# Expert loads, high-part casts, first sums and two split groups in a Macaron–Mamba–MoE kernel

## The chip, the cores and the metric

The kernel runs on one core of one Trainium2 chip. The metric is device microseconds (us) from the start to the end of the program on that core. Engines are named as in the profile: PE (matrix products), DVE (VectorE), ACT (ScalarE), POOL (GpSimd), SP (the queue that issues DMAs).

## The reference

The input x has 4 sequences of 1024 tokens with 128 features. Three residual steps follow each other, each on a layer norm of x: half a mixture of experts, a Mamba block, and the same mixture again.

```python
x = x + 0.5 * ffn(layernorm(x))
x = x + mamba(layernorm(x))
x = x + 0.5 * ffn(layernorm(x))

def ffn(x):                      # E = 8 experts, H = 128, F = 512, all of them run
    p = softmax(x @ w_router); q = softmax(x @ w_gating / 0.1)
    h = silu(x @ w_gate[e]) * (x @ w_up[e])          # for every e
    cw = p * q; cw = cw / (sum(cw) + 1e-9)
    return sum_e(cw[e] * (h @ w_down[e]))
```

The Mamba block projects to 256 channels, convolves over 4 tokens, makes step sizes and B and C from the result, runs a recurrence with 16 states per channel along the tokens, gates and projects back. All matrices are float32.

## The kernel before, in words

The 4096 tokens are cut into 8 blocks of 512. There are 16 mixture stages (8 blocks, twice) and 8 Mamba stages. `order` (L231) lists the mixture stages: the first mixture of block 0, of block 1, of block 2, and so on, mixed with second mixtures later. The Mamba work of a block runs beside the mixture of later blocks.

A mixture stage is 8 **groups**, one per expert; the groups are numbered through, so group 9 is expert 1 of the second stage. A group is two **halves** of 256 hidden features. This text names a half by the number in its tile names: half 0_8 is the one whose tiles are `pg`, `pu` and `h_0_8`, in block 0; expert 0 is halves 0_0 and 0_2, expert 2 is 0_8 and 0_10, expert 7 is 0_28 and 0_30; block 1 goes from 1_0 on. For each half:

- **gate** (`gate_part`, L595, and `half_products`, L628): 6 matmuls into the PSUM tile `pg`. Every float32 weight is kept as a high part `wh` and a low part `wl` in a faster format, as is the input (`xh`, `xl`). A product is `wh` by `xh`, `wh` by `xl`, `wl` by `xh` (L641 to L643). ACT then takes the silu of `pg` into `h` (L625).
- **up** (`up_part`, L646): 6 matmuls into `pu`, and DVE multiplies `h` by `pu` (L657). `pg` and `pu` have one buffer each: the next gate waits for the silu, the next up for the product.
- **down** (`down`, L676): in an ordinary group two plain float32 matmuls by `wd` (L722). A group listed in `SPL` (L41) is **split**: ACT casts `h` to a high part `hh` (L665), DVE subtracts to get `hl` (L667), the weight `wd` is parted in the same way into `wds` (L610 on ACT, L612 on DVE), and six fast matmuls (L697, L705) take the place of the two. `SPL` holds groups 1 to 10 and 113 to 126.

After a group's last down, ACT copies the PSUM tile `pd` to SBUF (`take`, L730, L735), and its result is multiplied by the routing weight `cwb` (L744) and added to `acc` (L747). The groups below `OWN` = 9 do that on DVE, later ones on POOL. `cwb` comes by DMA (`load_cw`, L584) from a DRAM tile `cd` that `cwt` (L553) writes after a transpose on PE (L556); it has 3 buffers, so the load of the fourth waits for the multiplication by the first.

**Weights.** `load_expert` (L276) issues three DMAs on SP for one expert, `w_gate` and `w_up` into `raw`, `w_down` into `wd`. `raw` has one buffer for experts 0, 3, 6 and two for the others, so expert 3 waits until `raw` of expert 0 has been read, expert 4 until that of expert 1 has. `split_expert` (L296) casts `raw` to `wh` (L298) and subtracts to get `wl` (L299), both on DVE.

**What sets the order.** The program has no loop at run time. While it is built, a class `Plan` (L54) keeps estimated clocks of the engines, and every instruction of the five queues is written out in the order that it decides. Time is counted in slots, 8 to a group. Lists of events have a slot each; line L1180 puts the load of expert e at `WL` = -5 slots and its parting at `WS` = +1 slot from slot 8(e-1). DVE work that may wait is handed to `plan.put` and taken when the planned DVE is free before the planned PE needs it; ACT work goes to `plan.act_put`. `plan.need` and `plan.act_need` force what has not yet been placed. Each queue runs in its order: an instruction that waits holds up all behind it on the same engine. A wait that the planner does not foresee is not avoided by it. `LOCK` (L47) and `on_pool` (L78) hold a model in which some DVE instructions and the POOL instructions exclude each other.

Around the change the layer norm of block 1 matters too (`mean_on_act`, L369): ACT sums (L379) and squares (L392), POOL makes `rs` and `nb` (L397 to L399), ACT writes `xn` (L414), PE transposes it (L438), ACT and DVE make `xh` and `xl` (L466, L471).

Of the kernel before, what the change touches and what calls it, by code (L numbers as in the profile page):

```python
# [8 lines left out]
F32 = mybir.dt.float32  # L9
F32R = mybir.dt.float32r  # L10
AF = mybir.ActivationFunctionType
ALU = mybir.AluOpType
# [25 lines left out]
POW = 4  # L38
WL = -5
WS = 1  # L40
SPL = (*range(1, 11), *range(113, 127))  # L41
OWN = 9
CWT0 = 11
FENDS = {0: 8, 1: 9, 9: 9, 15: 8}
# [128 lines left out]
def tile_macaron_mamba_moe(  # L173
# [20 lines left out]
    V, G, S, T = nc.vector, nc.gpsimd, nc.scalar, nc.tensor  # L194

    NB, L, H = x_in.shape
    E, _, F = w_gate.shape
# [20 lines left out]
    plan = Plan()  # L218
# [4 lines left out]
    def misc(name):  # L223
        if plan.reader in plan.spare:
            plan.act_need(plan.reader)
        plan.need(lambda: plan.reader is None or plan.reader[3])
        plan.wait_bank(name)
        return ps.tile([P, TB], F32, tag="misc", bufs=1, name=name)

    assert NBLK == 8  # L230
    order = [(1, 0), (1, 1), (1, 2), (1, 3), (2, 0), (1, 4), (2, 1), (1, 5), (2, 2), (1, 6), (1, 7)]  # L231
# [20 lines left out]
    def load_router():  # L252
        nc.sync.dma_start(out=wrg[:, 0:E], in_=w_router)
        nc.sync.dma_start(out=wrg[:, E:NE2], in_=w_gating)
# [16 lines left out]
        V.tensor_copy(wrg_h, wrg)  # L271
        V.tensor_tensor(wrg_l, wrg, wrg_h.bitcast(F32), ALU.subtract)

    wh, wl, wd, raws, cast = {}, {}, {}, {}, {}

    def load_expert(e):  # L276
        tag, bufs = (("xc", 1), ("y", 2))[e % 3 > 0]
        raw = sb.tile([P, 2, F], F32, tag=tag, bufs=bufs, name=f"wraw_{e}")
        nc.sync.dma_start(out=raw[:, 0, :], in_=w_gate[e])
        nc.sync.dma_start(out=raw[:, 1, :], in_=w_up[e])  # L280
        if e == 0:
            load_router()
        wd[e] = const.tile([P, FC * H], F32, name=f"wd_{e}")
        nc.sync.dma_start(
            out=wd[e].rearrange("p (c h) -> p c h", c=FC),
            in_=w_down[e].rearrange("(c p) h -> p c h", p=P),
        )
        wh[e] = const.tile([P, 2, F], F32R, name=f"wh_{e}")
        wl[e] = const.tile([P, 2, F], F32R, name=f"wl_{e}")
        raws[e] = raw  # L290
# [4 lines left out]

    def split_expert(e):  # L296
        raw = raws.pop(e)
        plan.put(lambda: V.tensor_copy(wh[e], raw), 0.69, plan.pe)  # L298
        cast[e] = plan.put(lambda: V.tensor_tensor(wl[e], raw, wh[e].bitcast(F32), ALU.subtract), 1.21, plan.pe)  # L299

    win_h = const.tile([P, 2 * DI], F32R, name="win_h")
    win_l = const.tile([P, 2 * DI], F32R, name="win_l")
# [289 lines left out]
    def split(s, e):  # L592
        return s * E + e in SPL

    def gate_part(s, c):  # L595
        d = ffn[s]
        kind, k = order[s]
        e, f = divmod(c, FC)
        assert e not in raws
        plan.need(lambda: "xl" in d)  # L600
        if e in cast:
            plan.need(lambda: cast[e][3])
        nm = f"{kind}_{k}_{c}"
        if f == 2 and s * E + e + 1 in SPL:
            x = (e + 1) % E
            ws = wds[s * E + e + 1] = {}
            ws["w"] = sb.tile([P, 2, FC * H], F32R, tag="big", bufs=BIG, name=f"wds_{s}_{e}")

            def high():
                S.copy(ws["w"][:, 0, :], wd[x])  # L610
                ws["wl"] = plan.put(
                    lambda: V.tensor_tensor(ws["w"][:, 1, :], wd[x], ws["w"][:, 0, :].bitcast(F32), ALU.subtract), 0.66, plan.act + 0.1  # L612
                )

            ws["wh"] = plan.act_put(high, 0.58, 0.0)
        g = s * GPS * FC + c
        pg = d["pg"] = half_products(s, c, 0, "pg", nm)
        t = plan.on_pe(1.38, silu_at.get(g - 2, 0.0))
        plan.act_fill(t + TOL - (1.29 if plan.table != "silu" else 0.0))
        if f == FC - 2:  # L620
            for w in list(ffn.values()):
                if "take" in w:
                    plan.act_need(w["take"])
        h = d["hp"] = sb.tile([P, 2, TB], F32, tag="h", bufs=HB, name=f"h_{nm}")
        S.activation(h, pg, AF.Silu)  # L625
        silu_at[g] = plan.on_act(1.06, t, "silu")
# [49 lines left out]
    def down(s, c):  # L676
        d = ffn[s]
        kind, k = order[s]
        e, f = divmod(c, FC)
        if f == 0:  # L680
            for o in list(ffn.values()):
                if "take" in o:
                    plan.act_need(o["take"])
            d["pd"] = ps.tile([P, TB], F32, tag="pd", bufs=1, name=f"pd_{kind}_{k}_{e}")
            if (s, e) == (len(order) - 1, E - 1):
                d["pds"] = d["pd"], misc("pd_end")
        h = d.pop(("h", c))
        cols = slice(f * H, (f + 1) * H)
        if len(h) == 2:
            ws = wds[s * E + e]  # L690
            w = ws["w"]
            if f % 2 == 0:
                plan.act_need(ws["wh"], d["hh", c])
                plan.need(lambda: ws["wl"][3])
                for q in range(2):
                    for i in range(2):
                        T.matmul(  # L697
                            d["pd"], w[:, i, (f + q) * H : (f + q + 1) * H], h[0][:, q, :],
                            start=(f + q + i == 0), stop=False,
                        )  # L700
                t = plan.on_pe(0.92, max(d["hh", c][4], ws["wl"][4]))
            else:
                plan.need(lambda: d["hl", c][3])
                for q in range(2):
                    T.matmul(  # L705
                        d["pd"], w[:, 0, (f + q - 1) * H : (f + q) * H], h[1][:, q, :],
                        start=False, stop=(f == FC - 1 and q == 1),
                    )
                t = plan.on_pe(0.46, d["hl", c][4])
        elif (s, e) == (len(order) - 1, E - 1):  # L710
            d["rest"] = d.get("rest", ()) + h
            if f % 2:
                for q in range(2):
                    part = slice(q * TB // 2, (q + 1) * TB // 2)
                    for g in (f - 1, f):
                        T.matmul(
                            d["pds"][q][:, 0 : TB // 2], wd[e][:, g * H : (g + 1) * H], d["rest"][g][:, part],
                            start=(g == 0), stop=(g == FC - 1),
                        )
            t = plan.on_pe(0.86, d["h_at", c])  # L720
        else:
            T.matmul(d["pd"], wd[e][:, cols], h[0], start=(f == 0), stop=(f == FC - 1))  # L722
            t = plan.on_pe(0.86, d["h_at", c])
        if f < FC - 1:
            return
        pd = d["pd"]
        edge = (s, e) == (len(order) - 1, E - 1)
        own = s * E + e < OWN or s == len(order) - 1

        def take():  # L730
            if e == 0:
                t = d["acc"] = sb.tile([P, TB], F32, tag="acc", bufs=2, name=f"acc_{kind}_{k}")
            else:
                t = sb.tile([P, TB], F32, tag="tmp", bufs=TMP, name=f"tmp_{kind}_{k}_{e}")
            S.copy(t, pd)  # L735

            def weight():
                cwb = d.pop(("cwb", e))
                at = max(plan.act, d["cwb_at", e])
                if e + 2 < E:  # L740
                    load_cw(s, e + 2)
                G_ = V if own else G
                put = (lambda f, cost, at: plan.put(f, 0.66, at)) if own else pool_put
                it = put(lambda: G_.tensor_tensor(t, t, cwb, ALU.mult), 1.25, at)  # L744
                if e > 0:
                    acc = d["acc"]
                    it = put(lambda: G_.tensor_tensor(acc, acc, t, ALU.add), 1.25, at)  # L747
                d["sum"] = it
                if e == E - 1:
                    d["tail"] = True  # L750
                    pool_run(None)

            if ("cwb", e) in d:
                weight()
            else:
                d.setdefault("late", []).append(weight)

        if edge:
            finish(d, d["pds"], k)
        else:  # L760
            d["take"] = plan.act_put(take, 0.58, t, True)
# [387 lines left out]
    def add(base, evs, wait=WAIT):  # L1149
        chains.append([(max(0, base + ev[0]), wait, *ev[1:]) for ev in evs])  # L1150
# [26 lines left out]
        add(START[k], mid, 99)  # L1177
        add(START[k], back, 40)
    for e in range(1, E):
        add(8 * (e - 1), [(WL, lambda e=e: load_expert(e)), (WS, lambda e=e: split_expert(e))])  # L1180
    add(8 * E, [(-24, load_mamba)])

    S.preload_act_table_set("silu_and_others")
# [3 lines left out]
    with tc.manual_schedule(engines={ET.PE, ET.Activation, ET.DVE, ET.Pool, ET.SP}):  # L1187
        half = 0
        while chains or done < nst:
            c = 2 * half  # L1190
            todo = []
            while done < min(nst, c - 2 * (done // FC in SPL)):
                todo.append(done)
# [47 lines left out]
```

## Time and profile before

| | us |
|---|---|
| three runs | 1262.1, 1262.14, 1264.05 |
| median | 1262.14 |
| the profiled execution | 1264.02 |
| its span, first to last instruction | 1262.2 |
| PE busy in the span | 1245.7 |
| DVE, ACT, POOL busy | 1141.8, 920.8, 705.8 |

The granted TensorE clock is full throughout. A matmul of 512 columns stands with 390 to 400 ns in the profile, but the next one starts 0.23 us later, because they overlap in the pipe. So the busy share of PE does not say how full it is: one looks at the starts. Twelve products and six split downs, one half of a split group, take 4.08 us from start to start where nothing waits; a half of an ordinary group takes 4.48 us. What a stretch takes beyond such steps is time that PE lost.

### The profile page before, as it was taken

The page shows a single profiled execution, that of the slowest core. Times are in us where ns is not written, and L with a number is a line of the kernel's source. Part 1 is how long each engine was busy: PE and PEld are TensorE (multiplying, and loading weights), DVE is VectorE, ACT ScalarE, POOL GpSimd, SP SyncE. Part 2 cuts the span into 40 slices and gives each one's busy share as a digit, 9 for nine tenths or more (in the row PEclk, how much of TensorE's full clock was granted, in tenths as well). Part 3 has the DMA queues.
Part 4 walks back from the last instruction along what each step waited for, and adds up shares of the span by engine and source line. Part 5 has one row for each costly group of instructions (what it writes and reads, how often), then busy time and mean ns, then how long its engine had stood idle before and what let it go on. Part 6 is the DMA issues. An engine that isn't in the chain of part 4 may idle for free. (4 is left out here: it accounts for less than half of the span.)

```text
span 1262.2 us, 14418 instructions
## 1 busy us (share of the span) xinstructions
PE 1245.7 (99%) x4800; PEld 861.0 (68%) x4800; DVE 1141.8 (90%) x1286; ACT 920.8 (73%) x1324; POOL 705.8 (56%) x557
## 2 busy tenths in 40 slices
PE   9999999999999999999999999999999999999998
PEld 6777666666666666666666666666666666667887
DVE  5986599999999999999999999999999999998676
ACT  6676887776778678877788787767876867656653
POOL 1012465767557656874576568656866575564400
PEclk9999999999999999999999999999999999999999
DMA  4501333243333433333433343433433433311110
GB/s 135 171 24 36 103 109 90 88 127 86 96 95 92 120 89 95 96 102 104 99 97 99 92 113 95 113 84 86 109 96 90 110 97 112 100 60 40 29 42 25
DMA packets 75387, 115.09 MB, mean 91 GB/s; under 512 B 7473, under 2 KB 23729, under 8 KB 75313
## 3 DMA queue, kind: packets, MB, share of 16 engines
q1 hardware_dynamic: 75312, 114.19, 33.4%
q8 instruction: 37, 0.61, 0.2%
q14 instruction: 38, 0.30, 0.1%
HBM read 109.71 MB, written 4.46 MB: 90 GB/s over the span
## 5 line engine op out<-in xcount | busy, mean ns | idle before, releaser
L722 PE MATMUL pd<-h,wd 128*128 128x512 f32 x824 | 391.5, 592 | 0.0
L657 DVE TENSOR_TENSOR h<-h,pu 128x1024 f32<-128x1024 f32 x256 | 310.9, 1214 | 69.8 <-PE pu L643 44.2
L1036 POOL TENSOR_TENSOR y_m<-y_m,da_m 128x1024 f32<-128x1024 f32 x128 | 309.7, 2420 | 107.6 <-DVE hb_m L1015 97.0
L625 ACT ACTIVATE h<-pg 128x1024 f32<-128x1024 f32 x256 | 262.9, 1027 | 139.4 <-PE pg L643 134.0
L641 PE MATMUL pg<-xh_f,wh 128*128 128x512 f32 x510 | 263.1, 516 | 1.5 <-DVE wh L298 0.7
L744 POOL TENSOR_TENSOR tmp<-tmp,cwb 128x512 f32<-128x512 f32 x98 | 132.1, 1348 | 206.2 <-issue 79.3
L722 PEld LDWEIGHTS pd<-h,wd 128*128 128x128 f32 x824 | 153.8, 188 | 107.0 <-issue 89.9
L641 PE MATMUL pu<-xh_f,wh 128*128 128x512 f32 x512 | 204.5, 399 | 2.5 <-DVE h L657 2.2
L643 PE MATMUL pg<-xh_f,wl 128*128 128x512 f32 x510 | 201.1, 394 | 0.5 <-DVE wl L299 0.5
L643 PE MATMUL pu<-xh_f,wl 128*128 128x512 f32 x512 | 200.4, 391 | 0.0
L642 PE MATMUL pu<-xl_f,wh 128*128 128x512 f32 x512 | 199.9, 390 | 0.0
L642 PE MATMUL pg<-xl_f,wh 128*128 128x512 f32 x510 | 199.4, 391 | 0.0
L1015 DVE TENSOR_TENSOR hb_m<-dx_m,bcb_m 128x1024 f32<-128x1024 f32 x128 | 173.2, 1353 | 2.2
L1021 DVE TENSOR_TENSOR_SCAN hb_m<-da_m,st_sb,hb_m 128x512 f32<-128x512 f32 x128 | 164.3, 1283 | 2.4
L1002 ACT ACTIVATE da_m<-dt_m,A_sb 128x512 f32<-128x512 f32 x256 | 164.0, 711 | 0.6
L1021 DVE TENSOR_TENSOR_SCAN hb_m<-da_m,hb_m 128x512 f32<-128x512 f32 x128 | 156.5, 1223 | 2.6
L1033 DVE TENSOR_TENSOR da_m<-hb_m,bcb_m 128x1024 f32<-128x1024 f32 x128 | 155.8, 1217 | 2.1
L641 PEld LDWEIGHTS pg<-xh_f,wh 128*128 128x128 f32 x510 | 96.0, 188 | 66.2 <-issue 26.8
L747 POOL TENSOR_TENSOR acc<-acc,tmp 128x512 f32<-128x512 f32 x98 | 130.2, 1329 | 7.7
L642 PEld LDWEIGHTS pg<-xl_f,wh 128*128 128x128 f32 x510 | 96.3, 189 | 46.8 <-issue 32.5
L641 PEld LDWEIGHTS pu<-xh_f,wh 128*128 128x128 f32 x512 | 96.1, 188 | 31.2 <-DVE h L657 11.5
L643 PEld LDWEIGHTS pg<-xh_f,wl 128*128 128x128 f32 x510 | 95.6, 188 | 23.0 <-DVE wl L299 0.9
(181 smaller groups left out, 1488.8 us busy)
## 6 DMA issues: line engine op xcount, KB each, us to landing
bcb_m<-bc_m SPq DMA_DIRECT2D x128, 512.0 KB
cwb<-cd_f SPq DMA_DIRECT2D x128, 256.0 KB
out_dram<-x SPq DMA_DIRECT2D x13, 256.0 KB
x<-in_L_attn_x_dram SPq DMA_DIRECT2D x8, 256.0 KB
wraw<-in_L_ffn_w_gate_dram SPq DMA_DIRECT2D x8, 256.0 KB
wraw<-in_L_ffn_w_up_dram SPq DMA_DIRECT2D x8, 256.0 KB
wd<-in_L_ffn_w_down_dram SPq DMA_DIRECT2D x8, 256.0 KB
cd_f<-ct_f SPq DMA_DIRECT2D x64, 4.0 KB
```

The costliest lines, as they stand in the source:

```text
L625: S.activation(h, pg, AF.Silu)
L641: T.matmul(o[:, q, :], wh[e][:, i, cols[q]], d["xh"], start=True, stop=False)
L642: T.matmul(o[:, q, :], wh[e][:, i, cols[q]], d["xl"], start=False, stop=False)
L643: T.matmul(o[:, q, :], wl[e][:, i, cols[q]], d["xh"], start=False, stop=True)
L657: V.tensor_tensor(h, h, pu, ALU.mult)
L722: T.matmul(d["pd"], wd[e][:, cols], h[0], start=(f == 0), stop=(f == FC - 1))
L744: it = put(lambda: G_.tensor_tensor(t, t, cwb, ALU.mult), 1.25, at)
L1002: S.activation(da[:, i, :], d["dt"][:, i, :], AF.Exp, scale=A_sb[:, i, n : n + 1])
L1015: mul = V.tensor_tensor(hb, d["dx"], bcb[:, 0:1, :].to_broadcast([P, ND, TB]), ALU.mult)
L1021: V.tensor_tensor_scan(hb[:, i, :], da[:, i, :], hb[:, i, :], 0.0 if first else st_sb[:, i, n : n + 1], ALU.mult, ALU.add,)
L1033: V.tensor_tensor(da, hb, bcb[:, 1:2, :].to_broadcast([P, ND, TB]), ALU.mult)
L1036: it = pool_put(lambda: G.tensor_tensor(d["y"], d["y"], da, ALU.add), 2.4, plan.dve)
```

## The change

Four things, in the code: expert 3 is loaded at -8 slots and expert 4 at -14 (both were at -5); a loaded expert's high part `wh` is cast by ACT and no longer by DVE, and only when that has been placed is the subtraction handed to DVE; of the groups below 9 only 7 and 8 keep their sums on DVE, so those of groups 0 to 6 go to POOL; groups 11 and 12 (experts 3 and 4 of block 1) are split as well. Two `need` lines keep the order right: a load of expert e above 3 is issued after the parting of expert e-3, and a gate forces the cast.

```diff
-SPL = (*range(1, 11), *range(113, 127))
+AHEAD = {3: -8, 4: -14, 5: -5, 6: -5}
+SPL = (*range(1, 13), *range(113, 127))
...
     def load_expert(e):
         tag, bufs = (("xc", 1), ("y", 2))[e % 3 > 0]
+        if e > 3:
+            plan.need(lambda: cast[e - 3] and cast[e - 3][3])
...
     def split_expert(e):
         raw = raws.pop(e)
-        plan.put(lambda: V.tensor_copy(wh[e], raw), 0.69, plan.pe)
-        cast[e] = plan.put(lambda: V.tensor_tensor(wl[e], raw, wh[e].bitcast(F32), ALU.subtract), 1.21, plan.pe)
+        def high():
+            S.copy(wh[e], raw)
+            cast[e] = plan.put(
+                lambda: V.tensor_tensor(wl[e], raw, wh[e].bitcast(F32), ALU.subtract), 1.21, plan.act + 0.1
+            )
+
+        cast[e] = None
+        high_at[e] = plan.act_put(high, 1.05, plan.pe)
...
         if e in cast:
+            plan.act_need(high_at[e])
             plan.need(lambda: cast[e][3])
...
-        own = s * E + e < OWN or s == len(order) - 1
+        own = (OWN - 3 < s * E + e < OWN) or s == len(order) - 1
...
-        add(8 * (e - 1), [(WL, lambda e=e: load_expert(e)), (WS, lambda e=e: split_expert(e))])
+        add(8 * (e - 1), [(AHEAD.get(e, WL), lambda e=e: load_expert(e)), (WS, lambda e=e: split_expert(e))])
```

Written out, the two programs have the same order on every engine from about the third stage on (some 230 us into the profile of before). Before that point it differs: 7 casts move from DVE to ACT, 13 instructions of the sums (7 multiplications, 6 additions) from DVE to POOL, and groups 11 and 12 add 6 casts on ACT, 6 subtractions on DVE, and 24 fast matmuls in place of 8 plain ones.

More of the change, by code (lines that the diff above doesn't have):

```diff
@@ L272, in split_router @@
         V.tensor_tensor(wrg_l, wrg, wrg_h.bitcast(F32), ALU.subtract)
-    wh, wl, wd, raws, cast = {}, {}, {}, {}, {}
+    wh, wl, wd, raws, cast, high_at = {}, {}, {}, {}, {}, {}
     def load_expert(e):
         tag, bufs = (("xc", 1), ("y", 2))[e % 3 > 0]
+        if e > 3:
+            plan.need(lambda: cast[e - 3] and cast[e - 3][3])
         raw = sb.tile([P, 2, F], F32, tag=tag, bufs=bufs, name=f"wraw_{e}")
```

## The prediction, made before the result was known

> **What bounds the kernel.** First the page's table of engines, then PE's waits in the first 230 us (below it the changed order is the old one), then windows.
>
> ```profile
> PE 1245.7 (99%) x4800; PEld 861.0 (68%) x4800; DVE 1141.8 (90%) x1286; ACT 920.8 (73%) x1324; POOL 705.8 (56%) x557
> ```
>
> PE is the bound from end to end: what PE loses, the program loses. The waits name where (us in total, times, longest):
>
> ```profile
> PE pd L705 <- DVE hl L667: 3.5, 2, 1.9
> ...
> PE pg L641 <- DVE wh L298: 0.7, 1, 0.7
> ...
> PE pg L643 <- DVE wl L299: 0.5, 1, 0.5
> ```
>
> All three name DVE, in stages 0 and 1. The windows (length, then busy us of each engine) show the stretches that I cut at gate starts:
>
> ```profile
> 24.36:40.34 15.98, 13.68 (x59) 10.32 (x59) 11.77 (x12) 9.09 (x14) 0.00 (x0) 1.00 0.66 214
> 40.34:66.15 25.81, 25.81 (x117) 21.08 (x115) 25.36 (x31) 17.58 (x24) 0.00 (x0) 1.00 0.48 128
> 66.15:82.00 15.85, 13.06 (x55) 9.90 (x54) 13.29 (x19) 12.70 (x23) 1.96 (x4) 1.00 0.05 17
> 82.00:113.79 31.79, 31.79 (x147) 25.86 (x145) 25.00 (x35) 23.59 (x41) 9.21 (x14) 1.00 0.16 50
> 113.79:148.76 34.97, 34.01 (x124) 22.10 (x123) 17.39 (x23) 22.92 (x31) 10.53 (x12) 1.00 0.28 79
> ```
>
> The reader sees DVE full in the second row (25.36 of 25.81) and POOL with nothing to do up to 66 us. Row one holds three halves, 12.69 us of work with a transposition of 0.45, so PE loses 3.3. Row three is three halves of 4.08: PE loses 3.6. The first loss starts with a late transfer (timelines of SP, DVE and PE; start, length):
>
> ```profile
> 26.31 0.37 SPq L279 DMA_DIRECT2D wraw<-in_L_ffn_w_gate_dram  x1
> ```
> ```profile
> 32.09 0.69 DVE L298 CAST wh<-wraw 128x1024 fp32r<-128x1024 f32 x1 [1.42 <-DMA wraw<-in_L_ffn_w_up_dram]
> ```
> ```profile
> 35.23 0.73 PE L705 MATMUL pd<-hl,wds 128*128 128x512 f32 x2 [1.91 <-DVE hl L667]
> ```
>
> Expert 3's load stood behind the write of `cd`, issued at 21.23 after a wait for ACT; DVE waits for it, and `hl` behind it makes PE wait.
>
> **Part 1, the early loads and the casts: 24 to 50 us.** I followed the changed order by hand with the durations above and these: silu 1.03, cast on ACT 1.05 (the row of `hh`, same shape; next start 0.95 later), product 1.22 (next 1.13 later), subtraction 1.23. Expert 3 can now be issued when `wl` of expert 0 ends (10.2), expert 4 after `wl` of expert 1 (15.1), both before `cd` at 21.2, so the transfers cost PE nothing. Expert 4's wait holds SP to 15.1, and three issues of 0.45 later SP is free for `cd`, which starts when it did.
>
> But the casts come late, because a forced cast is written just before its gate. ACT's first cast (expert 1, 11.6 to 12.6) fits: the exponentials behind it wait for DVE until 13.9 anyway. For expert 2 ACT's order is silu of half 0_6, then `wh`. ACT is full from 15.6, so that silu runs at about 23.7 (it was 23.2), the cast ends at 25.7, DVE's product 0_6 comes first and `wl` ends at 27.2. PE wants it at 24.84: a loss of **2.5**, of which 0.35 was lost before. Gate 0_10 starts at 30.9 (it was 28.80).
>
> Next a queue: on POOL the norm of block 1 (L397 to L399) now stands behind the first multiplication by `cwb`, which lands at 28.8 (DVE waited for it till then). POOL: 28.8 + 1.3, then 0.3 + 1.1 + 0.3 gives `nb` at 31.8, up to 33.0 if DVE's `wds` and `hl` hold it up. On ACT two `xn` wait for `nb`, and behind them the silu of 0_10, ready at 32.5: it ends at 33.9 to 34.9, then `wh` of expert 3, DVE's product 0_10, and `wl` at 36.3 to 37.3. PE wants it at 35.5: **0.9 to 1.8** lost. Gate 0_14 starts at 40.5 to 41.4 (40.34 before). From expert 4 on, the cast stands half a group ahead of its gate and nothing waits; the second gate of expert 4 starts at 49.8 to 50.7 against 49.70. The sum of the part: the loss of 3.3 goes, 3.3 to 4.3 take its place. I take **+0.5**. Bounds: -3.3, if no cast makes PE wait, to +1.9.
>
> **Part 2, DVE relieved: 50 to 82 us.** In a group of 8.16 us DVE had two products and two `hl` (4 x 1.13), `wl` 1.13, `wds` 0.60, `wh` 0.61, sums 1.33: 8.2, full. It loses 1.94. PE's 3.6 came from the order this forced: `wh` of expert 7 at 70.28 straight before its gate at 70.2, and `hl` of 0_26 after product 0_30 (80.16). Now `wh` of expert 7 stands two halves ahead, and `hl` of 0_26 before product 0_30: by hand at 76.5 for a need at 78.4. Gain 3.6, less 0.2 for product 0_30, which ends as up 1_0 wants it: **-3.4**; bounds -3.6 and 0.
>
> [...]
>
> ```profile
> 118.77 1.28 POOL L747 TENSOR_TENSOR acc<-acc,tmp 128x512 f32<-128x512 f32 x1
> ```
> ```profile
> 119.30 1.30 DVE L931 SCALAR_TENSOR_TENSOR cv_m<-xs_m,cw_sb,cv_m 128x512 f32<-128x512 f32 x1
> ```
>
> The DVE instruction takes 0.75 elsewhere and here 0.55 more: POOL ended at 120.05. At 109.63 it is POOL (1.84 for 1.30, against `hl`); the products of that time keep 1.22. POOL's two instructions a group, 2.6, meet `hl`, `wl`, `wds` (4.0 a group). DVE has 6.3 + waits of 0 to 2.6 in 8.16. In both rows a meeting costs about 0.55; I take two a group, 1.1: 7.4 of 8.16 fits.
>
> [...]
>
> POOL's new work stands ahead of the routing weights of block 1 (L547), and PE's transposition L556 is now written ahead of gate 1_2. By hand L547 ends at 82.6, PE comes at 83.0: **0**, bounds 0 and +1.3 (one sum held up).
>
> **Part 3, two split groups.** A half's down takes 1.36 for 1.72 (4.08 against 4.48 from start to start, the plain halves' pipe apart): four halves, **-1.44**. ACT gets 4 x 0.95 + 2 x 0.5, DVE 4 x 1.13 + 2 x 0.6 more; DVE is busy 17.39 of 34.97 there, ACT 22.92, so idle time hides them. Without that cover the 5.7 of DVE would stand ahead of the products. The convolution taps end some 2 us later after product 1_14, but the Mamba product L954 is now behind another down, and has 1.3 us left.
>
> **Part 4, what moves with them: 113.79 to 148.76.** Without the -1.44 this takes 33.5; by hand the changed order takes 32.1. Two losses shrink: PE's 0.41 around L497, which now comes ahead of L954, and the wait for the silu behind the first exponentials (gate at 148.76), as ACT's table loads meet PE later. I take **-0.9**, bounds -1.4 and +0.7. After that the order is the same and PE still bounds, so I carry the sum to the end.
>
> **Sum.** +0.5 - 3.4 + 0 - 1.44 - 0.9 = **-5.2**. The profiled execution took 1264.02, the highest but one of the four known times and 1.9 over the median; against itself the forecast is 1258.8, against the median of 1262.14 it is **1257.0**. I give the latter, as the steps are inside the span of 1262.2.
>
> **Rivals.**
> 1. *The waits only change places* (0.2). The casts make PE wait at more gates than two, and a DVE queue that now waits for ACT holds products: part 1 +1.9, part 2 half (-1.7), part 3 -1.44, part 4 0. Sum -1.2: 1260.9. For: the planner does not count PE's wait for a cast. Against: from expert 4 on it is half a group ahead.
> [...]
> 3. *The late cast costs nothing* (0.1): ACT reaches it before PE, part 1 is -3.3. Then -9.0: 1253.1. Against: ACT has no gap between 15.6 and 23.
> 4. *The loads do not come sooner* (0.02), as SP still stands behind something: then part 1 is 0, and the time is 1256.5, not to be told from the forecast.
>
> **How the numbers follow.** The forecast has 0.58 (with 4, 0.60). A measurement tells 0.2%, 2.5 us: faster is below 1259.6. Faster: forecast and 4 nearly whole (0.58), case 3 (0.1) and a little of case 1 (0.03): 0.71. Same: most of case 1 and the tail of the forecast, 0.20. Slower, above 1264.7: 0.09. The range runs from 1253.5, near case 3, to 1262.0, past case 1; case 2 is left out.
>
> **What would show it.** Right: DVE has idle time in 41 to 82; gate 0_14 still at about 40.5, with PE waiting on `wl` at gates 0_8 and 0_12; no wait on L705; gate 1_0 near 78.9 (82.00 before). [...]

## The result and the profile after

The changed kernel takes 1269.26 us (median of four runs, 1268.85 to 1269.88) against 1262.12 (1261.87 to 1264.05) for the kernel before on the same chip: a ratio of 1.0053, 95% interval 1.004 to 1.0066. It is slower. The forecast was 1257.0, faster. The profiled execution took 1268.85, span 1267.1; against before's profiled 1264.02 that is 4.8 more, where -5.2 was forecast. Among all the runs below one, of e6, took 1382.39 us at a mean clock of 0.85; e6's median counts it, its range and ratio do not.

In the changed kernel the lines of the code stand 9 or 10 lower than in the listing: silu L635, the three products L651 to L653, `hl` L677, the split downs L707 and L715, the plain down L732, the copy of `take` L745, POOL's sums L754 and L757, the Mamba product L964. The cast of `wh` on ACT is L302, `wl` on DVE L304.

The starts of gates in the two profiled executions tell where the time came from (us; half names as above):

| gate | before | after | difference | forecast start |
|---|---|---|---|---|
| 0_14 | 40.34 | 40.30 | -0.04 | 40.5 |
| 0_18 | 49.70 | 49.65 | -0.05 | 49.8 |
| 1_0 | 82.00 | 78.63 | -3.37 | 78.9 |
| 1_14 | 113.79 | 110.19 | -3.60 | |
| 1_20 | 134.05 | 130.22 | -3.83 | |
| 1_22 | 138.52 | 138.48 | -0.04 | |
| 1_24 | 143.01 | 148.70 | +5.69 | |
| 1_26 | 148.76 | 153.36 | +4.60 | 143.5 |

Up to 130 us the change does what it was forecast to do. Then it loses 8.4 us in two places within 20 us, and from 153 us to the end the difference stays between 3.9 and 5.2. PE's waits in the first 230 us of the profile after (us in total, times, longest) name both places:

```profile
PE pd L732 <- ACT tmp L745: 3.0, 1, 3.0
PE pd L707 <- ACT tmp L745: 2.7, 1, 2.7
PE pg L653 <- DVE wl L304: 1.4, 2, 0.7
PE dbl_m L964 <- DVE ex_f L515: 1.4, 1, 1.4
PE pg L651 <- ACT wh L302: 1.2, 1, 1.2
```

The old waits for `hl` are gone. Lines 3 and 5 are the late casts that Part 1 counted on. New are the first two: a down that waits for ACT to copy the tile `pd` of the group before. The windows of the same profile, cut at gate starts (length, then busy us of PE, its loads, DVE, ACT, POOL; granted clock):

```profile
25.48:40.30 14.82, 13.40 (x59) 10.47 (x59) 11.11 (x11) 10.62 (x17) 6.38 (x6) 1.00 0.47 131
40.30:66.10 25.80, 25.80 (x116) 21.08 (x115) 22.11 (x24) 20.81 (x27) 7.94 (x5) 1.00 0.43 117
66.10:78.63 12.53, 12.53 (x55) 10.06 (x54) 10.50 (x12) 12.01 (x24) 7.14 (x8) 1.00 0.06 21
78.63:110.19 31.56, 31.56 (x146) 25.92 (x145) 24.22 (x33) 24.77 (x43) 10.20 (x17) 1.00 0.17 50
110.19:153.36 43.17, 35.55 (x133) 25.24 (x131) 22.84 (x27) 26.81 (x35) 10.19 (x11) 0.92 0.22 64
```

DVE in row two fell from 25.36 to 22.11 of 25.8, and row three takes 0.3 more than three halves of 4.08, where it took 3.6 more before. The fifth row took 34.97 before and was to take 32.6 (34.97 - 1.44 - 0.9); it takes 43.17, with ACT busy 26.81 of that, far from full. The clock is below 1 in that row alone.

**What happens there.** `pd` has one PSUM buffer (the allocation in `down` says `bufs=1`). In a split group the last two downs stand behind `hl`, a half later than plain ones, so the copy of group 11 becomes possible later, and ACT's queue then has the Mamba block's softplus ahead of it, with its table load. ACT's timeline (start, length):

```profile
131.84 1.03 ACT L635 ACTIVATE h<-pg 128x1024 f32<-128x1024 f32 x1 [0.23 <-PE pg L653]
132.88 1.28 ACT L996 ACT_TABLE_LOAD   x1
134.17 1.06 ACT L996 ACTIVATE dt_m<-dt_m 128x1024 f32<-128x1024 f32 x1
135.14 0.57 ACT L745 COPY tmp<-pd 128x512 f32<-128x512 f32 x1
...
141.29 1.28 ACT L527 ACT_TABLE_LOAD   x1
...
142.84 2.54 ACT L1012 ACTIVATE da_m<-dt_m,A_sb 128x512 f32<-128x512 f32 x4
145.28 0.56 ACT L745 COPY tmp<-pd 128x512 f32<-128x512 f32 x1
```

PE's timeline shows the other side:

```profile
129.76 0.62 PE L715 MATMUL pd<-hl,wds 128*128 128x512 f32 x2
...
135.76 2.07 PE L707 MATMUL pd<-hh,wds 128*128 128x512 f32 x4 [2.66 <-ACT tmp L745]
137.63 1.05 PE L715 MATMUL pd<-hl,wds 128*128 128x512 f32 x2
140.05 1.07 PE L707 MATMUL pd<-hh,wds 128*128 128x512 f32 x4
140.96 0.61 PE L715 MATMUL pd<-hl,wds 128*128 128x512 f32 x2
145.90 3.56 PE L732 MATMUL pd<-h,wd 128*128 128x512 f32 x4 [2.97 <-ACT tmp L745]
```

`pd` of group 11 is complete at 130.4; the copy that frees it starts at 135.14, behind silu, table load and softplus; the first down of group 12 starts at 135.76. The same happens to group 12 (complete at 141.6, copied at 145.28, behind the first exponentials). And each wait costs more than itself: L707 takes 2.07 where the one at 140.05 takes 1.07, and L715 1.05 for 0.61, as the granted clock behind the wait is 0.50 (136 to 138 us). From 132.94, where L707 could have started, to gate 1_22 at 138.48 PE needs 5.54 for 1.37 of work: a wait of 2.82 and 1.35 of slow clock. From 142.77 to gate 1_24 at 148.70 it needs 5.93 for 1.72: 3.13 and 1.08. Together **8.4**.

In the kernel before, both groups are plain. Group 11's `pd` is complete at 128.2 and its copy starts at once, with softplus 9 us away; group 12's is complete at 139.1, as softplus ends. ACT's timeline before:

```profile
128.30 0.59 ACT L735 COPY tmp<-pd 128x512 f32<-128x512 f32 x1 [0.60 <-PE pd L722]
...
137.09 1.28 ACT L986 ACT_TABLE_LOAD   x1
138.38 1.06 ACT L986 ACTIVATE dt_m<-dt_m 128x1024 f32<-128x1024 f32 x1
139.35 0.57 ACT L735 COPY tmp<-pd 128x512 f32<-128x512 f32 x1
```

### The profile page after: what moved, and what is told of

It reads as the page before. It is cut to its first block, busy times and chain, and to the rows that moved or that the text cites. A ratio compares the mean times of both kernels' runs of the same rounds, so it can differ in the third digit from the quotient of the medians.

```text
span 1267.1 us, 14462 instructions
## 1 busy us (share of the span) xinstructions
PE 1246.5 (98%) x4808; PEld 864.0 (68%) x4808; DVE 1137.4 (90%) x1272; ACT 931.0 (73%) x1337; POOL 723.5 (57%) x570
## 5 line engine op out<-in xcount | busy, mean ns | idle before, releaser
L732 PE MATMUL pd<-h,wd 128*128 128x512 f32 x808 | 385.6, 594 | 3.0 <-ACT tmp L745 3.0
L635 ACT ACTIVATE h<-pg 128x1024 f32<-128x1024 f32 x256 | 262.6, 1026 | 143.2 <-PE pg L653 138.8
L754 POOL TENSOR_TENSOR tmp<-tmp,cwb 128x512 f32<-128x512 f32 x104 | 141.7, 1362 | 233.6 <-ACT tmp L745 87.6
L651 PE MATMUL pg<-xh_f,wh 128*128 128x512 f32 x510 | 263.4, 516 | 1.3 <-ACT wh L302 1.2
L732 PEld LDWEIGHTS pd<-h,wd 128*128 128x128 f32 x808 | 151.2, 189 | 108.2 <-issue 88.0
L651 PE MATMUL pu<-xh_f,wh 128*128 128x512 f32 x512 | 204.4, 399 | 1.8 <-DVE h L667 1.6
L653 PE MATMUL pg<-xh_f,wl 128*128 128x512 f32 x510 | 201.1, 394 | 1.4 <-DVE wl L304 1.4
L653 PE MATMUL pu<-xh_f,wl 128*128 128x512 f32 x512 | 200.4, 391 | 0.0
L757 POOL TENSOR_TENSOR acc<-acc,tmp 128x512 f32<-128x512 f32 x104 | 138.6, 1333 | 8.1
L651 PEld LDWEIGHTS pg<-xh_f,wh 128*128 128x128 f32 x510 | 96.3, 189 | 65.8 <-issue 27.1
L651 PEld LDWEIGHTS pu<-xh_f,wh 128*128 128x128 f32 x512 | 96.1, 188 | 30.1 <-DVE h L667 10.3
L653 PEld LDWEIGHTS pg<-xh_f,wl 128*128 128x128 f32 x510 | 95.6, 187 | 24.3 <-DVE wl L304 2.3
```

The source lines that it names most:

```text
L651: T.matmul(o[:, q, :], wh[e][:, i, cols[q]], d["xh"], start=True, stop=False)
L653: T.matmul(o[:, q, :], wl[e][:, i, cols[q]], d["xh"], start=False, stop=True)
```

## The experiments

Each timed kernel ran beside the kernel before, whose median was 1262.72 beside e1 to e4, 1262.75 beside e5 to e8 and 1262.59 beside e9 to e12; ratios are against these. My theory was the late copy of `pd`. The rivals: the split groups cost by themselves, wherever the copies stand; or casts and POOL's sums, by a new order, cost the time.

**e1: the changed kernel without the two more split groups.**

```diff
-SPL = (*range(1, 13), *range(113, 127))
+SPL = (*range(1, 11), *range(113, 127))
```

> The changed kernel without the split of groups 11 and 12; loads, casts and sums stay as changed. Theory T (the loss comes from the results of the two split groups: their copies out of the one PSUM tile pd stand on ACT behind the softplus and the exponentials, so PE waits for that tile and then runs at a lower granted clock): the 3.6 us that PE is ahead at gate 1_12 stay, about 1258.5, and no wait on the copy of pd. Rival S (the sums on POOL or the casts on ACT delay those copies): the waits of 2.7 and 3.0 are still there, 1266 or more.

Measured: 1261.92 (1260.09 to 1263.53), ratio 0.9992 [0.9983, 1.0]. No wait for `pd` is left, and the time is 7.3 under the changed kernel's 1269.26 (by ratios, 0.9992 for 1.0053): without the split groups the loss is gone. But it is 3.4 over what I expected, so something else eats the gain of Part 2.

**e2: the kernel before with the two more split groups alone.** (In `SPL`, the line of the change.)

> The kernel before with only the split of groups 11 and 12 added. Theory T: the order on ACT around the softplus is the same as in the changed kernel, so the same loss of about 8.2 us from gate 1_14 on comes to the kernel before: about 1270.3, with the granted clock below full in that stretch. Rival S: without casts on ACT and sums on POOL the copies come in time, and the four shorter downs give 1 to 1.4: about 1261.

Measured: 1270.7 (1269.02 to 1274.29), ratio 1.0062 [1.005, 1.0075]. PE waits 2.66 and 2.98 for the copy L735, as in the changed kernel (2.66 and 2.97). The split groups alone bring the whole loss; it does not need the rest of the change.

**e3: in the changed kernel ACT copies `pd` of group 11 ahead of softplus.** One instruction of ACT's queue is moved; the second `settle()`, ahead of the exponentials, moves nothing here.

```diff
+    def settle():
+        for w in list(ffn.values()):
+            if "take" in w:
+                plan.act_need(w["take"])
...
+            if k == 0:
+                settle()
             S.activation(d["dt"], d["dt"], AF.Softplus)
...
+                if k == 0 and q == 0:
+                    settle()
```

> The changed kernel with one instruction moved: on ACT the copy of group 11's pd is written ahead of the softplus and its table load, not behind; all other orders are the same. Theory T: PE's wait of 2.7 ahead of the downs of group 12 falls to about 0.6, the clock stays full there (1.35 us), so 3.4 less: 1265.8; the second wait of 3.0 stays. Rival L (the added casts and subtractions load ACT and DVE, and the place of the copy does not matter): no change, 1269. Rival C (the clock falls by itself and makes the loss): the clock falls in the same place and the time stays.

Measured: the profiled execution 1265.69, as expected; but the median is 1269.44 (1265.69 to 1270.63), ratio 1.0047 [1.0035, 1.0059], 3.6 over what I expected and no gain on the changed kernel. In the profile the first wait falls from 2.66 to 0.29, and the second stays:

```profile
PE pd L732 <- ACT tmp L745: 3.5, 1, 3.5
```

The other runs differ from the profiled one in the clock: it has a mean of 0.999, they have 0.994 to 0.996. The moved instruction takes its wait away in the profile. Why the clock falls further in the other five, which have no trace, is not shown.

**e4: both copies first.** As e3, and the first exponentials of the Mamba block come a slot later, so that the copy of group 12 stands ahead of them.

```diff
-            mid += [(n0 + 8 * int(SPR * q) + w, two, turn)]
+            first_two = k == 0 and q == 0
+            mid += [(n0 + 8 * int(SPR * q) + w, two, late_turn if first_two else turn)]
```

> As the one before, and the first burst of exponentials is planned one slot later, so that the copy of group 12's pd stands ahead of it. Theory T: the second wait goes too, 3.1 and 1.1 for the clock: about 1261.5, with full clock throughout; what is left against the 1258.5 without the split is the wait of 1.4 for the bank of the Mamba product L954 (L964 in the changed kernel) and 0.6 behind it. Rival L: no change, 1269.

Measured: 1261.59 (1260.05 to 1263.42), ratio 0.9985 [0.9977, 0.9994]. With all the work of the change still there, the order of two copies on ACT is worth 7.7 us (1269.26 - 1261.59). ACT's timeline now has each copy ahead of the table load:

```profile
134.54 0.58 ACT L745 COPY tmp<-pd 128x512 f32<-128x512 f32 x1
135.14 1.28 ACT L1004 ACT_TABLE_LOAD   x1
...
139.73 0.58 ACT L745 COPY tmp<-pd 128x512 f32<-128x512 f32 x1
140.33 1.28 ACT L527 ACT_TABLE_LOAD   x1
```

So the first theory holds, by e1, e2 and e4 together: the split costs the time where the two copies come late, and not by itself. But e4 is no better than e1. The stretch from gate 1_14 to 1_26 takes 34.79 (before: 34.97), not 32.6. What is left of the loss is at gate 0_8, where ACT's cast makes PE wait 1.17 and DVE's subtraction 0.73 more. In e4's profile the clock falls there too (2-us windows):

```profile
26.00:28.00 2.00, 1.27 (x6) 0.80 (x5) 1.02 (x1) 0.00 (x0) 0.54 (x1) 0.96 0.59 207
28.00:30.00 2.00, 2.00 (x6) 1.52 (x5) 0.00 (x0) 1.46 (x3) 1.92 (x3) 0.50 0.23 52
30.00:32.00 2.00, 2.00 (x8) 1.57 (x7) 0.83 (x1) 1.01 (x2) 0.20 (x2) 0.69 0.95 131
```

Half 0_8 takes 6.8 there and 5.23 in the profile after, with the same waits and the clock at 1. The runs of e4 stand accordingly in three levels: 1260.1 to 1260.5 (mean clock 1.0), 1261.6 to 1262.0 (0.998 to 0.999), 1263.4 (0.997).

The next four take the rest apart.

**e5: the kernel before with the sooner loads alone.**

```diff
+AHEAD = {3: -8, 4: -14, 5: -5, 6: -5}
...
+        if e > 3:
+            plan.need(lambda: cast[e - 3][3])
...
-[(WL, lambda e=e: load_expert(e))
+[(AHEAD.get(e, WL), lambda e=e: load_expert(e))
```

> The kernel before with one thing changed: experts 3 and 4 (and, by a little, 5 and 6) are loaded sooner; all casts stay on VectorE, no more split groups, sums as before. If before's profiled execution shows its usual run, the late transfer of expert 3 (VectorE waits for it until 32.09) costs it 2.3 to 2.9 us and that goes: about 1259.5, gate 0_14 near 37.5 to 38.0 against 40.34, and no wait of the correction product for hl in stage 0. If the profiled execution, which is 1.9 over before's usual run, is that much over because the transfer landed late in it alone, the gain is 1.0 or less: 1261.1 or more.

Measured: 1260.71 (1260.34 to 1262.27), ratio 0.9985 [0.9976, 0.9994]. In the profile the loads are worth 3.26: half 0_10 takes 4.08 for 7.00, and nothing is given back later. By the medians they are worth 2.0 (e12 says why the profiles may show more).

**e6: the kernel of e1 with all casts back on DVE**, so the loads and POOL's sums alone. In `split_expert`:

```diff
+        if True:
+            plan.put(lambda: V.tensor_copy(wh[e], raw), 0.69, plan.pe)
+            cast[e] = plan.put(lambda: V.tensor_tensor(wl[e], raw, wh[e].bitcast(F32), ALU.subtract), 1.21, plan.pe)
+            return
```

> The kernel of e1 (no more split groups) with all casts of the experts' high parts back on VectorE: the sooner loads and GpSimd's sums alone. If ScalarE's late casts cost what e1's profile shows at gates 0_8 and 0_12 (waits of 1.2, 0.7 and 0.7, and 1.6 of slow clock behind them), those 3 to 4 us go and the relief of VectorE in stage 0 is kept but for 0.6 a group: about 1258.0, and the clock stays at 1.0 around 26 to 32. If the falls of the clock come with the shorter time itself and not with those waits, about 1260.5 and a fall elsewhere. If VectorE needs the casts' 0.6 a group, the loss ahead of gate 1_0 comes back in part: 1260 or more.

Measured: 1262.64 (1261.4 to 1263.53), ratio 0.9992 [0.9983, 1.0001]. My first branch was wrong, the last one right: against e5's profile it loses 1.4 ahead of gate 0_18 and wins only 0.4 of the 3.6 between 0_18 and 1_0. PE's waits between 40 and 90 us:

```profile
PE pu L657 <- DVE h L673: 2.1, 2, 1.5
PE lt_f L499 <- DVE xl_f L485: 1.0, 1, 1.0
```

DVE's timeline shows a cast of 1.79 for 0.69 and a subtraction of 2.21 for 1.21, each beside a sum of POOL that is longer than its usual 1.3 as well (54.69 to 56.55 and 64.06 to 66.01):

```profile
55.30 1.79 DVE L302 CAST wh<-wraw 128x1024 fp32r<-128x1024 f32 x1
...
64.89 2.21 DVE L303 TENSOR_TENSOR wl<-wraw,wh 128x1024 fp32r<-128x1024 f32 x1
```

**e7: the kernel of e4 with all casts back on DVE** (same edit).

> The kernel of e4 (two more split groups, with the copies of groups 11 and 12 ahead of softplus and of the first exponentials) with all casts back on VectorE. By the theory of the late casts e4's 1261.6 loses 3 to 4: about 1258.0, with no wait for pd, for wh or wl above 0.3 in stage 0, and the split groups worth 0.3 or less against e6. If the split groups are worth the 1.44 of the prediction once pd is free in time, 1.4 below e6.

Measured: 1262.81 (1261.91 to 1265.82), ratio 1.0001 [0.9992, 1.001]; 1258.0 was wrong for the same reason as in e6, whose wait for `h` (2.1) is here too, with one of 1.7 for `xl`.

**e8: the kernel of e4 with the casts of experts 1 to 3 on DVE, those of 4 to 7 on ACT** (`if e < 4:` for `if True:`).

> The kernel of e4 with the casts of experts 1, 2 and 3 on VectorE and those of experts 4 to 7 on ScalarE. If only the first casts are late, and VectorE is full from 41 us on, this takes both gains: 0.5 to 2 below e7, about 1257.0. If VectorE has room for the casts once GpSimd has the sums, the same as e7 within 0.5.

Measured: 1258.97 (1258.91 to 1259.43), ratio 0.9968 [0.9956, 0.9981]. It takes both gains, 3.8 below e7 where 0.5 to 2 was forecast, but 2 us short of the time that I expected: the runs lie within 0.5, and the clock stays at 1 in the profile. Only the first casts were late, and only the later ones relieve DVE where it is full (25.36 of 25.81 us in the profile of before). The split groups' own balance is in this profile: gate 1_14 to 1_26 takes 34.80, for 34.97 before. PE's waits there:

```profile
PE dbl_m L976 <- DVE ex_f L520: 1.4, 1, 1.4
...
PE v_m L997 <- DVE dbs_m L985: 0.6, 1, 0.6
PE pd L713 <- ACT tmp L751: 0.3, 1, 0.3
```

**e9: the kernel of e8 without the two more split groups** (`SPL` as in e1).

> The kernel of e8 (casts of experts 1 to 3 on VectorE, 4 to 7 on ScalarE, GpSimd's sums, sooner loads) with groups 11 and 12 no longer split, so that the order from 106 us on is the old one. By e8's profile the split groups win 2.5 by gate 1_16 and give it back in waits of 1.4, 0.6 and 0.3 (banks misc and pd): worth 0.2, so this takes 1259.2. If the split is worth its 1.44, 1260.4.

Measured: 1259.83 (1258.88 to 1260.42), ratio 0.9975 [0.9967, 0.9984]. The stretch takes 34.97. The intervals of e8 and e9 overlap: what the two split groups are worth, once the copies stand right, is not above what these runs can tell. In the profiles it is 0.2 at gate 1_26 and nothing at the end (spans of 1257.6 and 1257.5).

**e10: the kernel of e9 with the sums of groups 0 to 6 back on DVE.**

```diff
-        own = (OWN - 3 < s * E + e < OWN) or s == len(order) - 1
+        own = s * E + e < OWN or s == len(order) - 1
```

> The kernel of e9 with the sums of groups 1 to 6 back on VectorE: sooner loads and ScalarE's casts of experts 4 to 7 are left. If ScalarE's casts alone relieve VectorE between 50 and 82 us, and GpSimd's sums only put the norm of block 1 late (a loss of 1.2 ahead of gate 0_18 in e8), this is faster than e9 by 1.2: 1258.0. If VectorE needs to be rid of the sums as well (1.33 a group), the old loss of 2.8 to 3.3 ahead of gate 1_0 is there again: 1260.7, as e5.

Measured: 1257.33 (1256.7 to 1259.02), ratio 0.9958 [0.9944, 0.9971]. Without POOL's sums the stretch from 0_18 to 1_0 takes 28.70, for 32.30 before, 32.31 in e5 and 29.46 in e9. Its window row:

```profile
48.52:77.22 28.70, 28.70 (x128) 23.73 (x127) 26.16 (x32) 24.67 (x39) 3.21 (x6) 1.00 0.25 65
```

DVE has 2.5 us to spare there with the sums on it. e10 is e5 with the four later casts on ACT. By the medians these are worth 3.4 (1260.71 and 1257.33; the intervals of the ratios lie apart), and in this stretch they bring all of Part 2's 3.6. The rest of the profile, the longest of e10's five runs, is no such comparison. Ahead of gate 0_18 it is 2.1 behind e5 (48.52 and 46.43), as DVE's first sum waits 2.28 for `cwb`, 0.36 in e5 (see e12). Behind gate 1_0 the planner has written another order: 27.64 to gate 1_12 for 25.78 before, then 38.49 to gate 1_26 for 40.98.

**e11: the kernel of e9 with the sums of groups 0 to 3 alone back on DVE.**

```diff
+        own = s * E + e < 4 or OWN - 3 < s * E + e < OWN or s == len(order) - 1
```

> The kernel of e9 with the sums of groups 1 to 3 alone back on VectorE, so that the norm of block 1 no longer stands behind a multiplication that waits for its weights on GpSimd's queue, while groups 4 to 6 are summed on GpSimd. By e8's profile the half at gate 0_14 then takes 4.1 instead of 5.8 and 1.2 us stay won to the end: 1258.0. If the wait comes from VectorE's own queue and not from GpSimd's, the same as e9.

Measured: 1257.71 (1257.29 to 1259.62), ratio 0.9962 [0.995, 0.9975]. The time is right, the reason I gave is not, and half 0_14 takes 4.97 for 5.75 in e9, not the 4.1 that I expected. In e9 POOL has `nb` of block 1 at 24.0, well ahead of its sums. What is late is DVE. First POOL's timeline in e9, then DVE's:

```profile
36.53 1.30 POOL L763 TENSOR_TENSOR acc<-acc,tmp 128x512 f32<-128x512 f32 x1
```
```profile
36.95 1.96 DVE L309 TENSOR_TENSOR wl<-wraw,wh 128x1024 fp32r<-128x1024 f32 x1
38.83 0.68 DVE L485 TENSOR_TENSOR xl_f<-pt_f,xh_f 128x512 fp32r<-128x512 f32 x1
```

The subtraction begins at 36.95 and ends 1.1 after POOL's sum does, 0.74 over its usual 1.22. Behind it `xl` is late, and PE waits 0.68 for `xl`. That POOL's sum costs this wait is read from e9's trace alone; e11 does not test it. There no POOL sum runs at that time, but DVE does the sum itself and makes `xl` later still, from 39.36. PE has no such wait because the planner has put the products that read `xl` (L499, the router's logits) behind the up products: they start at 40.10, for 39.56 in e9. e10 and e11 are the best versions found; which of them is better the runs do not tell.

**e12: the kernel before once more.**

> The kernel before once more, for a second profile. If its first profile, at 1264.02, shows a late transfer of expert 3 that its usual runs (1262.0) do not have, VectorE's wait at about 32 is shorter here and half 0_10 takes 5 to 6 us instead of 7.00. If the difference lies elsewhere, half 0_10 takes 7.0 again.

Measured: 1263.92 in the profiled execution. Half 0_10 takes 7.22 (7.00 in the first profile), with the same wait of DVE for expert 3 (1.69, first 1.42). So the late transfer is in both profiles. That leaves open why both profiled executions stand at about 1264.0 while some six in ten of before's runs lie between 1261.6 and 1262.8. It is not the clock alone, which is 1.000 in both and 1.0 in runs of both levels. Only profiled executions have a trace, so I cannot say where before's quicker runs save 1.9 us.

The traces hold a candidate: the write of `cd`, whose landing SP awaits before it issues the first load of `cwb`. SP's timeline in before, then in e5:

```profile
21.23 1.35 SPq L563 DMA_DIRECT2D cd_f<-ct_f  x4
25.38 0.83 SPq L588 DMA_DIRECT2D cwb<-cd_f  x2
```
```profile
20.93 1.35 SPq L566 DMA_DIRECT2D cd_f<-ct_f  x4
23.36 4.19 SPq L591 DMA_DIRECT2D cwb<-cd_f  x4
```

From the first issue of the write to the first of `cwb` it takes 4.15 and 4.09 us in the two profiles of before, 4.22 in e2, 4.21 in e10 and 3.94 in e7, and 2.41 to 2.44 in the other nine. e9, e10 and e11 are written alike up to there, so this differs between executions. In before the load of expert 3 stands behind it on SP. If `cd` lands 1.7 sooner in the quicker runs, that load is issued as much sooner; no trace of such a run shows it. As it stands, the difference means that gains read between two profiles are up to 2 us larger than those between medians, as e5 shows (3.26 and 2.0).

## Why the prediction was wrong, point by point

- **Part 1 was right in the profile, in part by luck.** +0.5 was forecast; gate 0_18 stands at -0.05. But `cwb`, put at 28.8 as before, was there at 27.3 (POOL's first multiplication starts at 27.34): the write of `cd` took 2.43 in this execution and 4.15 in before's. PE waits for ACT's casts and DVE's subtractions at gates 0_8 (1.17 and 0.72; 2.5 forecast, 2.36 by its own 27.2 less 24.84) and 0_12 (0.69; 0.9 to 1.8 forecast), and the norm on POOL stands behind `cwb` as worked out. The cost of the first wait was too small where the clock falls behind it, which adds 1.6 in the profiles of e1 and e4 (in the profile after it did not fall there). Rival 3, a late cast that costs nothing, put the loads alone at -3.3; e5 has -3.26.
- **Part 2 was right in size and wrong in what carried it.** -3.4 was forecast, -3.32 came (0_18 to 1_0). The sums were to make room on DVE, as POOL has "nothing to do up to 66 us". The runs show that the sums on POOL bring none of it (e10), that they bring 0.4 when the casts stay on DVE (e6), and, by e9's trace alone, that one of them costs 0.7 where DVE is in a hurry. The casts of experts 4 to 7 carry the gain (e10 against e5). Meetings of POOL and DVE were put at 1.1 a group; between 41 and 79 us of the profile after, three of DVE's subtractions take 1.95, 2.30 and 1.73 for 1.22, 2.3 in all over four groups and thus about 0.6 a group. At most 0.3 of it reached PE: the product that stands behind the subtraction of 2.30 ends at 71.64, the up of half 0_28 starts at 71.70, and that half takes 4.37 for 4.08. Case 2, which the range leaves out, has each of POOL's sums hold DVE for all its 1.3; no run shows that. What they show are these 2.3 over four groups, and in e6, where the casts stay on DVE, the cast and the subtraction that took 1.1 and 1.0 longer.
- **Part 3 is the step that failed:** "DVE is busy 17.39 of 34.97 there, ACT 22.92, so idle time hides them." The share of idle time says how much work fits, not where it stands. I priced the added casts and subtractions and did not follow the copy that a later last down delays. It is on a one-buffer tile, in a queue with softplus, exponentials and four table loads of 1.28 in these 15 us. In place of -1.44 for the split groups the two waits cost +8.4. It was to be seen beforehand: `pd` with `bufs=1` in the code, softplus and exponentials on ACT in the trace of before, where group 12's copy stands right behind softplus.
- **The "1.3 us left" of the Mamba product** was wrong as well. It waits 1.40 here. Product and router logits share the one buffer of `misc`, and the logits' reader on DVE stands behind an `hl` that the split added. With 0.6 at L985 and 0.3 at `pd`, that is why even well-ordered split groups gain 0.2 and not 1.44 (e8, e9).
- **Part 4's 32.1 "by hand" fails with Part 3**: the order I followed had no wait for `pd` in it. The signs named for a right prediction all came, as far as gate 1_0. None of them looked behind it, at ACT's copies.
- **The sum.** Against the profiled executions the forecast is off by 10.0: 8.4 for the two copies, the rest mainly split groups that do not gain. (Rival 4's terms give 1256.4, not 1256.5.) By the medians it is off by 12.3: before's median is 1.9 under its profiled execution, after's 0.4 over.
- **The clock** was not priced at all. The profile of before, at a clock of 1.000, shows no fall to price it from, and the prediction counted each wait of PE at its own length. The runs show that the falls vary (e4's levels), and that each of the four falls seen in windows (one in e1, one in e4, two in the profile after) comes to 3.4 us at half speed. Which idle stretch brings one they do not show: the clock fell after waits of 2.66 and 2.97 us in the profile after and 3.53 in e3's, and in those of e1 and e4 after 1.17 and 0.73 us with two matmuls between them. After 1.17 and 0.72 us in the profile after it did not fall.

## What to carry to other kernels

When a change delays the last write of a single-buffered tile, find the instruction that empties it and read what stands ahead of that in its own queue. The busy share of that engine says nothing about it. Work taken from a full engine helps where that engine sets the pace, and it can be taken too early (ACT's casts of the first three experts) or to an engine beside whose work the relieved one takes longer (POOL's first sums: 1.79 for 0.69 in e6). And try the parts one by one: of four parts, two carried a gain (the loads and the later casts), and dropping the others left 1257.3 of 1262.6.

## What the runs showed of the hardware

- **A short wait of PE cost twice here.** After idle stretches of 1.9 us in two pieces (e1 and e4), 2.66 and 2.97 (after) the granted clock went to 0.50, which cost 1.6, 1.35 and 1.08 us more. In the three rows of e4 the missing shares of the clock (0.04, 0.50 and 0.31 of 2 us, over 0.5) come to 3.4 us at half speed; so do those of e1 (0.16, 0.50 and 0.20 in the same windows). Three windows of the profile after show one such fall whole, again 3.4 us (length, busy, and the clock as third number from the end):

```profile
134.00:136.00 2.00, 0.24 (x1) 0.24 (x2) 1.17 (x2) 1.97 (x4) 0.22 (x1) 0.86 0.85 225
136.00:138.00 2.00, 2.00 (x5) 1.57 (x6) 0.49 (x1) 1.00 (x1) 1.92 (x2) 0.50 0.42 163
138.00:140.00 2.00, 2.00 (x8) 1.59 (x7) 0.00 (x0) 0.00 (x0) 0.98 (x1) 0.79 0.35 104
```

- **Whether it falls varied from run to run of one program.** The times come in levels about 1.7 us apart (e1: 1260.1, 1261.8, 1263.5). In e4 the mean clock of a run goes with its level; in e1 the lower two levels both have runs at 0.999, and the two levels of the kernel before are not told by it. Runs of e3 range over 5 us, at mean clocks of 0.994 to 0.999. A wait of 1.9 in the kernel before (35.23; 2.2 in its second profile) brought no fall in either, at a mean clock of 1.000.
- **The gap behind a small write was 1.7 us longer in some executions than in others.** The first load of `cwb` follows the write of `cd` by 2.4 us in nine profiles and by 3.9 to 4.2 in five (e12).
- **Table loads on ACT took 1.28 each** and are part of what a queued copy waits for: one load and one softplus, 2.3 in all, stood ahead of group 11's.
